# Attention with sign-weight feed-forward on one core: float32r rows for the feed-forward, another opening, and another share of the sums for GpSimd

## The chip, the cores and the metric

The kernel runs on one core of a Trainium2 chip. The metric is the device time of one execution in microseconds. A core has five engines that matter here: TensorE (PE in the profile), VectorE (DVE), ScalarE (ACT), GpSimd (POOL) and the queue engine SyncE (SP), which issues DMAs. Each works through its own instructions in order, and they wait for one another by semaphores. TensorE writes its products to eight banks of PSUM, and a bank is free again when the engine that reads it has finished.

## The reference

```python
def _L0_attn_ref(x, Wq, Wk, Wv):           # x: (4, 2048, 512), 16 heads of 32
    q = (x @ Wq.T).reshape(N, S, H, hd).transpose(0, 2, 1, 3)
    k = (x @ Wk.T).reshape(N, S, H, hd).transpose(0, 2, 1, 3)
    v = (x @ Wv.T).reshape(N, S, H, hd).transpose(0, 2, 1, 3)
    energy = jnp.einsum('nhqd,nhkd->nhqk', q, k)
    attn = jax.nn.softmax(energy / jnp.sqrt(jnp.float32(hd)), axis=3)
    out = jnp.einsum('nhql,nhld->nhqd', attn, v)
    return out.transpose(0, 2, 1, 3).reshape(N, S, D)

def _L0_ffn_ref(x, weights, scale, bias):
    w = (weights >= 0.0).astype(x.dtype) * 2.0 - 1.0
    y = jnp.einsum('bsi,oi->bso', x, w)
    y = y * scale + bias
    return jnp.clip(y, -100.0, 100.0)

x = _layernorm(x + _L0_attn_ref(x, Wq, Wk, Wv), axis=-1)
x = _layernorm(x + _L0_ffn_ref(x, weights, scale, bias), axis=-1)
```

Everything is float32. The feed-forward has the shape of one 512 x 512 matrix of signs, followed by a scale and a bias for each output column.

## The kernel before

**Work and steps.** A *group* `n` is one batch and four of the sixteen heads, so there are 16 groups, four to a batch. A *block* is 512 queries of one group (four blocks a group), and a *step* is one chunk of 128 keys for one block: 16 steps a block, 64 a group, 1024 in all. The program is one long list of steps, written out in full. In each step TensorE makes the scores of the chunk for four heads at once (`scores`, L300 and L306: first a bf16 product that puts minus the row maximum into the bank, then the f32 product of keys and queries), ScalarE takes exp (L313) into a tile `p` of 128 x 2048, and every second step TensorE multiplies two such tiles with the values (`weighted`, L324).

**Row maxima ahead.** The maxima are computed by a separate pass: `max_unit` (L248, L255, L267) makes the scores of 128 queries against 512 keys for four heads, and VectorE reduces each of the four banks to a maximum, the fourth one by way of a copy by ScalarE. One such unit stands in each step, for the step that comes `LEAD` = 22 steps later; sixteen units make a block's maxima, which `max_parts` collects and SP transposes by a DMA. So 22 units are done before the first scores.

**The denominators.** GpSimd adds up the tiles `p` of a block (`add_up`, L344): chunk 0 and 1 in its first instruction, then one chunk in each, up to chunk 14, so 14 additions a block. In `denominators` TensorE multiplies chunk 15 and then the sum of the other fifteen with a column of ones (`ones_times`, L350), which adds over the 128 keys. A tile `p` is taken from `ppool`, which has four buffers; a buffer is free when the value product and the addition have both read it. The very last block has a split of its own.

**Projections, feed-forward and finishing.** Into the odd steps a planner (`plan`) puts *big* tasks (pieces of the projections of the next group, L206, and pieces of the feed-forward) and *small* ones (transposes by TensorE); into the even steps it puts *col* tasks, such as the denominators. Each task has a first and a last step; the planner runs twice, the second time with the number of big tasks a group as a quota. In its units a piece of keys or queries weighs 2, a piece of values or feed-forward 1, and an odd step in the middle holds 2. Once a batch's attention is done, its rows are finished in the steps of the next batch (`Finish`): a first layer norm, `turn` (four transposes, L518, and ScalarE's copy, L524), `ffn` (L532 and three VectorE operations, L537, L538 and L540), a second layer norm and the store. The rows of the last batch are finished near the end (`finish_last`) and after it (`finish_end`). `take` and `give` keep a model of when each bank is free.

**The feed-forward.** The weights were turned into signs and multiplied with the scale before the start (`sign_weights`, GpSimd). A tile of 128 rows is done in three pieces of 172, 172 and 168 columns, each four f32 matmuls; in the last two blocks in one piece of 512.

**The opening.** Wk and Wq are loaded as a whole on ScalarE's queue and transposed; x comes tile by tile (128 rows, 256 KB) into a stage of three buffers on SP's queue, and each transpose issues the next load. Then come keys, queries and units, and Wv and the feed-forward weights are loaded meanwhile (`load_rest`).

Of the kernel before, what the change touches and what calls it, by code (L numbers as in the profile page):

```python
# [12 lines left out]
BF16 = mybir.dt.bfloat16  # L13
AF = mybir.ActivationFunctionType
# [6 lines left out]
def kernel(  # L21
# [13 lines left out]
    P = 128  # L35
# [14 lines left out]
    THIRDS = (0, 172, 344, D)  # L50
    W = 2 * P
    LEAD = NT + 6

# [4 lines left out]
    stage = ctx.enter_context(tc.tile_pool(name="stage", bufs=3))  # L58
    mpool = ctx.enter_context(tc.tile_pool(name="mpool", bufs=2))
    cpool = ctx.enter_context(tc.tile_pool(name="cpool", bufs=2))  # L60
# [5 lines left out]
    ppool = ctx.enter_context(tc.tile_pool(name="ppool", bufs=4))  # L66
# [54 lines left out]
    def load_weight(w, name):  # L121
        if name == "ws":
            raw = xpool.tile([P, DC, D], F32, tag="xg", name="raw_ws")
        else:
            raw = ppool.tile([P, DC, D], F32, tag="p", name=f"raw_{name}")
        rows = w.rearrange("(c p) i -> p c i", p=P)
        for cols in [slice(0, D)] if name in ("wv", "ws") else [ts(ic, P) for ic in range(DC)]:
            nc.scalar.dma_start(out=raw[:, :, cols], in_=rows[:, :, cols])
        return raw

    wT = {}

    def transpose_weight(name, ic):
        if ic == 0:
            wT[name] = const.tile([P, DC, D], F32, name=f"{name}T")
        i = take()
        pt = cols_of(i, DC, P)
        for oc in range(DC):
            nc.tensor.transpose(pt[:, oc, :], raws[name][:, oc, ts(ic, P)], ident)  # L139
        runs("full", 0.44)  # L140
        nc.scalar.copy(wT[name][:, ic, :].rearrange("p (c o) -> p c o", c=DC), pt)
        give(i, "ACT", 0.6)

    def sign_weights():

        ws = raws["ws"]
        nc.gpsimd.tensor_scalar(ws, ws, 0.0, 2.0, ALU.is_ge, ALU.mult)
        for oc in range(DC):
            nc.gpsimd.tensor_scalar(
                ws[:, oc, :], ws[:, oc, :], 1.0, scale_t[:, oc : oc + 1], ALU.subtract, ALU.mult  # L150
            )

    raws = {n: load_weight(w, n) for n, w in (("wk", wk), ("wq", wq))}
    scale_t = const.tile([P, DC], F32, name="scale_t")
    bias_bc = const.tile([P, D], F32, name="bias_bc")

    def load_rest():
        for n, w in (("wv", wv), ("ws", w_ffn)):
            raws[n] = load_weight(w, n)
        nc.sync.dma_start(out=scale_t, in_=ffn_scale.rearrange("(c p) -> p c", p=P))  # L160
        nc.sync.dma_start(out=bias_bc, in_=ffn_bias.partition_broadcast(P))
# [3 lines left out]
    xin = {}  # L165
# [14 lines left out]
    coming = [(b, g, j) for b in range(B) for g in range(NQB) for j in range(NTQ)]  # L180

    def load_x():
        if coming:
            b, g, j = coming.pop(0)
            xin[b, g, j] = stage.tile([P, D], F32, tag="xs", name="xs")
            nc.sync.dma_start(out=xin[b, g, j], in_=x[b, ds(g * QB + j * P, P), :])

    def transpose_x(b, g, j):
        if j == 0:
            xT[b, g] = xtpool.tile([P, DC, QB], F32, tag="xT", name=f"xT_{b}_{g}")  # L190
        xs = xin.pop((b, g, j))
        i = take()
        pt = cols_of(i, DC, P)
        for c in range(DC):
            nc.tensor.transpose(pt[:, c, :], xs[:, ts(c, P)], ident)  # L195
        runs("full", 0.44)
        nc.scalar.copy(xT[b, g][:, :, ts(j, P)], pt)
        give(i, "ACT", 0.6)
        load_x()
# [138 lines left out]

    def add_up(n, qb, kc, p, before):
        if kc == 1:  # L340
            acc[n, qb] = apool.tile([P, HG, QB], F32, tag="acc", name="acc")
        if 0 < kc < (NT // 2 if is_last(n, qb) else NT - 1):
            a = acc[n, qb]
            nc.gpsimd.tensor_tensor(a, before if kc == 1 else a, p, ALU.add)  # L344
        if kc == NT - 1:
            last_p[n, qb] = p
# [20 lines left out]
    def denominators(n, qb):  # L367
# [3 lines left out]
        else:  # L371
            b = take()
            ones_times(b, last_p.pop((n, qb)), True, False)
# [73 lines left out]
    class Finish:  # L447
# [66 lines left out]
        def turn(self, j):  # L514
# [5 lines left out]
            if self.b < B - 1:  # L520
                self.nT[j] = work.tile([P, DC, P], F32, tag="nT", name="nT")
            else:
                self.nT[j] = self.room[:, j, :].rearrange("p (c q) -> p c q", c=DC)
            nc.scalar.copy(self.nT[j], pt)  # L524
            give(i, "ACT", 0.6)

        def ffn(self, j, third):
            cols = slice(0, D) if third is None else slice(THIRDS[third], THIRDS[third + 1])
            i = take()
            py = ps[:, i, : cols.stop - cols.start]  # L530
            for c in range(DC):
                nc.tensor.matmul(  # L532
                    py, lhsT=self.nT[j][:, c, :], rhs=wT["ws"][:, c, cols],
                    start=(c == 0), stop=(c == DC - 1),
                )
            runs("full", 6.8e-3 * (cols.stop - cols.start))
# [4 lines left out]
            give(i, "DVE", 0.5 + 3.1e-3 * (cols.stop - cols.start))  # L541

        def make_room(self):

            if self.g < NQB // 2:
                t = kpool.tile([P, S], F32, tag="kT", name="room") if self.g == 0 else shared[0]
                shared[:] = [t]
                self.room = t.rearrange("p (j d) -> p j d", j=NTQ)
            else:
                self.room = xpool.tile([P, NTQ, D], F32, tag="xg", name="room")  # L550
# [30 lines left out]
    def finish(b, qb, a, every, w, lag):  # L581
# [6 lines left out]
        for j in range(NTQ):  # L588
# [3 lines left out]
            for k in range(3):  # L592
                task("big", t + 2, t + w, f.ffn, j, k, after=turned)
# [8 lines left out]
    def finish_last(qb, last):  # L602
# [5 lines left out]
        at(a + 1, f.make_room)  # L608
# [4 lines left out]
        for j in range(NTQ):  # L613
# [6 lines left out]
            for k in [None] if late else range(3):  # L620
                task("big", by if late else t + 2, by, f.ffn, j, k, after=turned)
# [8 lines left out]
    def finish_end(qb, last):  # L630
# [10 lines left out]
        at(total + 3, f.make_room)  # L641
# [12 lines left out]
    start = -LEAD - 5  # L654
    for ic in range(DC):
        task("small", -10, -2, transpose_weight, "wv", ic)
        task("small", 4, 60, transpose_weight, "ws", ic)
    at(-LEAD - 2, load_rest)
    at(-8, sign_weights)
    for n in range(N):  # L660
# [3 lines left out]
        for i in range(NQB):  # L664
# [3 lines left out]
            last = -LEAD + NTQ * i - (2 if i else 6) if n == 0 else first + (12, 12, 11, 8)[i]  # L668
# [7 lines left out]
        for t in range(NT):  # L676
            i, j = divmod(t, NTQ)
            after = turned[b, i, j]
            task("big", max(s0 - STEPS + 2, ready[i], -6), latest(i, s0 + t), project_v, n, t,
                 after=after)  # L680
            if j % 2 == 0:
                continue
            free = s0 - STEPS + 1 if n else start
            task("big", max(free, ready[i]), s0 - LEAD - 1 + i * (1 if n else NTQ),
                 project_k, n, t // 2, after=after)
            last = s0 + NT * i - LEAD + NTQ * (j - 1) - 1
            if n == 0 and i == 0:
                last = -LEAD - 2 + j
            task("big", max(s0 + NT * (i - 2), start), latest(i, last), project_q, n, t // 2,
                 after=after)  # L690
        for qb in range(NQB):
            first = s0 + NT * qb
            last = first + NT - 1
            ahead[first - 5] = n, qb
# [9 lines left out]
            if g == NG - 1:  # L704
# [3 lines left out]
                else:  # L708
                    (finish_end if is_last(n, qb) else finish_last)(qb, last)

# [6 lines left out]
    def plan(quota=None):  # L717
# [9 lines left out]
        while any(len(gone[kind]) < len(tasks[kind]) for kind in tasks):  # L727
# [5 lines left out]
            elif s % 2:  # L733
                most = {"small": 1, "big": 2}
# [46 lines left out]
    for _ in range(3):  # L781
        load_x()
    for name in ("wk", "wq"):
        for ic in range(DC):
            transpose_weight(name, ic)
# [6 lines left out]
    while s <= max(*chosen, *behind):  # L792
# [10 lines left out]
        later = None  # L803
        if 0 <= s + LEAD < total:
            n, at_n = divmod(s + LEAD, STEPS)
# [14 lines left out]
        if later is not None:  # L820
            later()
        if now is not None:
# [42 lines left out]
```

## Time and profile before

| | before |
|---|---|
| median of 3 runs | 4386.38 us (4384.66 to 4386.73) |
| profiled execution, its own time | 4386.25 us |
| its span, first to last instruction | 4384.5 us |
| mean granted TensorE clock | 0.998 |
| busy: PE, weight loads | 4345.0 us (99%), 2135.5 us (49%) |
| busy: DVE, ACT, POOL | 3315.9 us (76%), 2999.3 us (68%), 4083.3 us (93%) |
| GpSimd additions (L344) | 825 + 64, 4.54 us each |
| first scores (L300) start | 84.4 us |

The profile shows one execution. Its span is 1.75 us shorter than the same execution's time, and that time is within 0.2 us of the median. An f32 matmul leaves two records on TensorE, and so does its weight load; a bf16 matmul and a transpose leave one. The busy time of TensorE is not a measure of how well it works, because the ends of matmuls are modelled: how long a matmul really holds TensorE is read from one start to the next. In the chain of waits the pieces are laid end to end, so a group of matmuls there has about the time that it holds the engine.

### The profile page before, as it was taken

To read this page: it belongs to the slowest core of one execution; us is meant where nothing else is said; L and a number is where in the kernel's file an instruction comes from. 1 tells how busy PE (TensorE), PEld (TensorE's weight loads), DVE (VectorE), ACT (ScalarE), POOL (GpSimd) and SP (SyncE) were. 2 spreads that over 40 slices of the span, in tenths; PEclk is the share of its full clock that TensorE was granted. 3 is DMA by queue.
4 is the path that set the end of the run, shared out by engine and by line. 5 is a ranking of instruction groups with operands and counts; after the bars stand their busy time and mean duration, and the time that the engine had idled before them with its cause. 6 is when DMAs were issued, how large, how long until landed. Compare 5 with 4: busy or idle time off the path is not lost.

```text
span 4384.5 us, 89302 instructions
## 1 busy us (share of the span) xinstructions
PE 4345.0 (99%) x36092; PEld 2135.5 (49%) x36092; DVE 3315.9 (76%) x5908; ACT 2999.3 (68%) x6173; POOL 4083.3 (93%) x940
## 2 busy tenths in 40 slices
PE   9999999999999999999999999999999999999998
PEld 5444444444454454455445454455544545455443
DVE  6777777777777777777777777777777777777774
ACT  4666666676667667676676766767667676767665
POOL 3999999999999999999999999999999999999993
PEclk9999999999999999999999999999999999999999
DMA  2000000010001000011000100001100000001101
GB/s 88 11 10 14 11 14 10 12 39 22 21 13 27 13 23 20 11 45 36 21 20 11 33 10 21 23 10 49 25 20 21 20 21 23 20 11 33 24 23 49
DMA packets 263351, 101.41 MB, mean 23 GB/s; under 512 B 169372, under 2 KB 239004, under 8 KB 262936
## 3 DMA queue, kind: packets, MB, share of 16 engines
q1 hardware_dynamic: 257656, 91.50, 8.6%
q8 instruction: 282, 4.62, 0.4%
q10 hardware_dynamic: 5280, 4.19, 0.3%
q14 instruction: 133, 1.09, 0.1%
HBM read 54.26 MB, written 33.02 MB: 20 GB/s over the span
## 4 chain that ended last, share of the span: by engine, by line
PE 91%; POOL 6%; DVE 1%; ACT 1%; issue 1%; DMA 0%; ACTq 0%; POOLq 0%; DVEq 0%
PE ps L324 20%; PE ps L248 19%; PE ps L306 19%; PE ps L206 15%; PE ps L300 8%; POOL acc L344 6%; PE ps L532 5%; PE ps L350 3%; PE ps L391 1%; PE ps L195 1%; PE ps L518 1%; ACT p L313 1%; DVE part L255 1%; DMA xs<-in_L_attn_x_dram 0%; PE ps L139 0%
## 5 line engine op out<-in xcount | busy, mean ns | idle before, releaser
L344 POOL TENSOR_TENSOR acc<-acc,p 128x2048 f32<-128x2048 f32 x825 | 3743.7, 4538 | 102.8 <-ACT p L313 42.6
L313 ACT ACTIVATE p<-ps 128x512 f32<-128x512 f32 x4096 | 2114.8, 602 | 1136.0 <-PE ps L306 1108.2
L255 DVE TENSOR_REDUCE part<-ps 128x1 f32<-128x512 f32 x3072 | 1933.0, 683 | 774.6 <-PE ps L248 774.2
L248 PE MATMUL ps<-kT,qT 32*128 32x512 f32 x8192 | 1114.3, 590 | 0.2 <-DVE xg_last L434 0.2
L306 PE MATMUL ps<-qT,kT 32*128 32x512 f32 x8192 | 1073.3, 591 | 0.0
L324 PE MATMUL ps<-p,vv 128*32 128x512 f32 x8192 | 983.4, 598 | 1.8 <-ACT p L313 1.8
L248 PEld LDWEIGHTS ps<-kT,qT 32*128 32x128 f32 x8192 | 542.8, 184 | 381.0 <-issue 194.5
L255 DVE TENSOR_REDUCE part<-moved 128x1 f32<-128x512 f32 x1024 | 691.9, 676 | 3.3 <-ACT moved L267 3.2
L267 ACT COPY moved<-ps 128x512 f32<-128x512 f32 x1024 | 631.0, 616 | 22.1 <-PE ps L248 18.0
L324 PEld LDWEIGHTS ps<-p,vv 128*32 128x32 f32 x8192 | 220.2, 109 | 686.9 <-issue 345.9
L300 PE MATMUL ps<-negm,ones_bf 32*128 32x512 bf16 x4096 | 443.1, 384 | 4.9 <-ACT p L313 2.9
L306 PEld LDWEIGHTS ps<-qT,kT 32*128 32x128 f32 x8192 | 405.8, 184 | 44.3 <-issue 27.5
L336 DVE TENSOR_TENSOR oT<-ps,oT 128x512 f32<-128x512 f32 x448 | 309.7, 691 | 97.4 <-PE ps L324 59.2
L344 POOL TENSOR_TENSOR acc<-p 128x2048 f32<-128x2048 f32 x64 | 290.8, 4544 | 96.0 <-ACT p L313 95.8
L300 PEld LDWEIGHTS <-ones_bf 32*128 32x128 bf16 x4096 | 105.6, 91 | 551.0 <-issue 522.3
L206 PEld LDWEIGHTS ps<-wvT,xT 128*128 128x128 f32 x2048 | 250.9, 191 | 80.3 <-ACT p L313 75.6
L206 PE MATMUL ps<-wvT,xT 128*128 128x128 f32 x2048 | 279.2, 280 | 0.3 <-ACT p L313 0.2
L206 PE MATMUL ps<-xT,wqT 128*128 128x256 f32 x1024 | 248.8, 386 | 2.7 <-ACT p L313 2.7
L206 PE MATMUL ps<-xT,wkT 128*128 128x256 f32 x1024 | 248.7, 387 | 0.0
L206 PEld LDWEIGHTS ps<-xT,wkT 128*128 128x128 f32 x1024 | 184.9, 190 | 68.8 <-ACT p L313 47.0
L206 PEld LDWEIGHTS ps<-xT,wqT 128*128 128x128 f32 x1024 | 184.5, 190 | 66.6 <-ACT p L313 44.9
L532 PEld LDWEIGHTS ps<-wsT,nT 128*128 128x128 f32 x1152 | 167.8, 189 | 94.2 <-ACT p L313 93.3
(75 smaller groups left out, 1722.4 us busy)
## 6 DMA issues: line engine op xcount, KB each, us to landing
xs<-in_L_attn_x_dram SPq DMA_DIRECT2D x64, 256.0 KB
xc<-in_L_attn_x_dram SPq DMA_DIRECT2D x60, 256.0 KB
res<-xc SPq DMA_DIRECT2D x60, 256.0 KB
xg<-res SPq DMA_DIRECT2D x12, 1024.0 KB
out_dram<-xg SPq DMA_DIRECT2D x12, 1024.0 KB
xg_last<-res SPq DMA_DIRECT2D x4, 768.0 KB
out_dram<-xg_last SPq DMA_DIRECT2D x3, 1024.0 KB
raw_wk<-in_L_attn_Wk_dram ACTq DMA_DIRECT2D x4, 256.0 KB
```

Source lines behind the costliest of these rows:

```text
L206: nc.tensor.matmul(pp, lhsT=lhs(c), rhs=rhs(c), start=(c == 0), stop=(c == DC - 1))
L248: nc.tensor.matmul(ps[:, banks[h], :], lhsT=qT[n, qb][rows, ts(qc, P)], rhs=kT[n][rows, ts(kb, QB)], start=True, stop=True,)
L255: nc.vector.tensor_reduce(part[:, qc, h : h + 1, kb], src, AX.X, ALU.max, negate=True)
L267: nc.scalar.copy(moved, ps[:, banks[-1], :])
L300: nc.tensor.matmul(ps[:, banks[h], :], lhsT=ones_bf[rows, :], rhs=negm[n, qb][rows, :], start=True, stop=False,)
L306: nc.tensor.matmul(ps[:, banks[h], :], lhsT=kT[n][rows, ts(kc, P)], rhs=qT[n, qb][rows, :], start=False, stop=True,)
L313: nc.scalar.activation(p[:, h, :], ps[:, banks[h], :], AF.Exp, scale=SM_SCALE)
L324: nc.tensor.matmul(pb[cols, :], lhsT=vv[n][:, kc, cols], rhs=p[:, h, :], start=(i == 0), stop=(i == 1),)
L336: nc.vector.tensor_tensor(outs[n, qb], pb, outs[n, qb], ALU.add)
L344: nc.gpsimd.tensor_tensor(a, before if kc == 1 else a, p, ALU.add)
L350: nc.tensor.matmul(ps[h * HD : (h + 1) * HD, b, :], lhsT=ones, rhs=p[:, h, :], start=start, stop=stop,)
L532: nc.tensor.matmul(py, lhsT=self.nT[j][:, c, :], rhs=wT["ws"][:, c, cols], start=(c == 0), stop=(c == DC - 1),)
```

## The change

Five things change together.

1. **Feed-forward.** `turn` makes two tiles in float32r: ScalarE copies the transposed rows into `high`, and VectorE subtracts `high` from the same bank into `low`. `ffn` multiplies both with the weights, which are now pure signs in float32r, in two halves of 256 columns (one piece of 512 in the last two blocks): eight matmuls a half into one bank. The scale is a tile of its own and a fourth VectorE operation. The room that the last batch used for its turned rows goes.
2. **The sums.** In every second block of batches 1 to 3 GpSimd adds 13 chunk pairs instead of 14, and TensorE multiplies two single chunks with ones, not one. The very last block keeps its split.
3. **The opening.** The first 128 rows of Wk and Wq, then all 16 tiles of x of batch 0, are loaded at once, x into four of the buffers of `ppool`. The other rows of Wk, Wq and Wv come through the stage and are transposed in the group before they are needed.
4. **The lead.** 18 units, not 22, stand ahead of the first scores (`LEAD0`); in the first steps of the run every second step holds a second unit until the lead is 22 again. An odd step with a second unit holds one big task less.
5. **Buffers.** `ppool` has five, not four; `stage` two, not three; `cpool` (columns of x for the attention sum) one, not two.

```diff
-    THIRDS = (0, 172, 344, D)
+    HALF = D // 2
     LEAD = NT + 6
+    LEAD0 = NT + 2
-    stage = ctx.enter_context(tc.tile_pool(name="stage", bufs=3))
+    stage = ctx.enter_context(tc.tile_pool(name="stage", bufs=2))
-    cpool = ctx.enter_context(tc.tile_pool(name="cpool", bufs=2))
+    cpool = ctx.enter_context(tc.tile_pool(name="cpool", bufs=1))
-    ppool = ctx.enter_context(tc.tile_pool(name="ppool", bufs=4))
+    ppool = ctx.enter_context(tc.tile_pool(name="ppool", bufs=5))
...
+    def transpose_weight(name, g):
+        if g == 0:
+            wT[name] = const.tile([P, DC, D], F32, name=f"{name}T")
+        raw = xin.pop((name, g))
+        i = take()
+        pt = cols_of(i, DC, P)
+        for ic in range(DC):
+            nc.tensor.transpose(pt[:, ic, :], raw[:, ts(ic, P)], ident)
+        runs("full", 0.44)
+        nc.scalar.copy(wT[name][:, :, ts(g, P)], pt)
+        give(i, "ACT", 0.6)
+        if g:
+            load_next()
...
         nc.gpsimd.tensor_scalar(ws, ws, 0.0, 2.0, ALU.is_ge, ALU.mult)
-        for oc in range(DC):
-            nc.gpsimd.tensor_scalar(
-                ws[:, oc, :], ws[:, oc, :], 1.0, scale_t[:, oc : oc + 1], ALU.subtract, ALU.mult
-            )
+        nc.gpsimd.tensor_scalar(ws, ws, 1.0, 0.0, ALU.subtract, ALU.add)
...
+    def load_first():
+        first = ppool.tile([P, DC, D], F32, tag="p", name="first_w")
+        for i, name in enumerate(("wk", "wq", "wv")):
+            xin[name, 0] = first[:, i, :]
+        for name in ("wk", "wq"):
+            nc.scalar.dma_start(out=xin[name, 0], in_=rows_of[name][ds(0, P), :])
+        for g in range(NQB):
+            t = ppool.tile([P, NTQ, D], F32, tag="p", name="first_x")
+            for j in range(NTQ):
+                xin[0, g, j] = t[:, j, :]
+                nc.sync.dma_start(out=t[:, j, :], in_=x[0, ds(g * QB + j * P, P), :])
+
     def load_rest():
+        nc.scalar.dma_start(out=xin["wv", 0], in_=wv[ds(0, P), :])
+        raws["ws"] = xpool.tile([P, DC, D], F32, tag="xg", name="raw_ws")
+        nc.scalar.dma_start(out=raws["ws"], in_=w_ffn.rearrange("(c p) i -> p c i", p=P))
+        nc.sync.dma_start(out=scale_bc, in_=ffn_scale.partition_broadcast(P))
         nc.sync.dma_start(out=bias_bc, in_=ffn_bias.partition_broadcast(P))
...
+    def chunks_added(n, qb):
+        if is_last(n, qb):
+            return NT // 2
+        return NT - 1 if n < NG or qb % 2 == 0 else NT - 2
+
     def add_up(n, qb, kc, p, before):
-        if 0 < kc < (NT // 2 if is_last(n, qb) else NT - 1):
+        if 0 < kc < chunks_added(n, qb):
             a = acc[n, qb]
             nc.gpsimd.tensor_tensor(a, before if kc == 1 else a, p, ALU.add)
-        if kc == NT - 1:
-            last_p[n, qb] = p
+        elif kc >= NT - 2:
+            last_p[n, qb] = last_p.get((n, qb), []) + [p]
...
-            ones_times(b, last_p.pop((n, qb)), True, False)
+            for k, p in enumerate(last_p.pop((n, qb))):
+                ones_times(b, p, k == 0, False)
...
-            if self.b < B - 1:
-                self.nT[j] = work.tile([P, DC, P], F32, tag="nT", name="nT")
-            else:
-                self.nT[j] = self.room[:, j, :].rearrange("p (c q) -> p c q", c=DC)
-            nc.scalar.copy(self.nT[j], pt)
-            give(i, "ACT", 0.6)
+            high = work.tile([P, DC, P], F32R, tag="high", name="high")
+            low = work.tile([P, DC, P], F32R, tag="low", name="low")
+            nc.scalar.copy(high, pt)
+            spend("ACT", 0.6, clock["PE"] + 0.2)
+            nc.vector.tensor_tensor(low, pt, high, ALU.subtract)
+            give(i, "DVE", 0.7)
+            self.nT[j] = high, low
...
-        def ffn(self, j, third):
+        def ffn(self, j, half):
-            for c in range(DC):
-                nc.tensor.matmul(
-                    py, lhsT=self.nT[j][:, c, :], rhs=wT["ws"][:, c, cols],
-                    start=(c == 0), stop=(c == DC - 1),
-                )
-            runs("full", 6.8e-3 * (cols.stop - cols.start))
+            for k, part in enumerate(self.nT[j]):
+                for c in range(DC):
+                    nc.tensor.matmul(
+                        py, lhsT=part[:, c, :], rhs=wT["ws"][:, c, cols],
+                        start=(k == c == 0), stop=(k == 1 and c == DC - 1),
+                    )
+            runs("full", 3.4e-3 * wide)
+            nc.vector.tensor_tensor(py, py, scale_bc[:, cols], ALU.mult)
             nc.vector.tensor_tensor(py, py, bias_bc[:, cols], ALU.add)
...
-            ahead[first - 5] = n, qb
+            ahead[first - (5 if first else 2)] = n, qb
...
+    def units(s):
+        def first(s):
+            return min(max(s + min(LEAD0 + max(s, 0) // 2, LEAD), 0), total)
+
+        return range(first(s), first(s + 1))
...
-                most = {"small": 1, "big": 2}
+                most = {"small": 1, "big": 3 - len(units(s))}
```

## The prediction

> **What bounds the kernel now.** I read the page's busy rows first, then the chain of waits for two stretches apart (the first batch, and the three later ones), then the timeline for the pace of single instructions, and last the chain of the opening and of the end.
>
> The windows of batch 0 and of the next two (columns: stretch; length; busy time of PE, weight loads, DVE, ACT, POOL; clock, DMA):
>
> ```profile
> 84.00:1116.00 1032.00, 1024.62 (x8644) 484.45 (x8639) 764.13 (x1282) 705.87 (x1451) 1004.80 (x222) 1.00 0.07 17
> 1116.00:2187.00 1071.00, 1069.83 (x9028) 530.59 (x9023) 829.71 (x1485) 744.74 (x1531) 1026.51 (x233) 1.00 0.09 22
> 2187.00:3257.00 1070.00, 1069.52 (x9026) 530.43 (x9024) 829.79 (x1489) 746.70 (x1536) 1024.35 (x233) 1.00 0.09 22
> ```
>
> Each row is one batch, 16 blocks of 16 steps: a block takes 64.5 us in batch 0 and 66.9 us later. PE is busy all but 1 us of a later batch, at full clock, but POOL is above 95% too. The chain tells them apart (first line: 110 to 1116 us, second: 1116 to 4250 us):
>
> ```profile
> by line: POOL acc L344 24.9%; PE ps L324 16.6%; PE ps L306 15.6%; PE ps L248 15.3%; PE ps L206 14.2%; PE ps L300 6.8%; PE ps L350 2.4%; issue 1.6%; ACT p L313 1.0%; PE ps L195 0.9%; PE ps L391 0.8%; PE ps L139 0.1%; POOLq L344 0.1%
> by line: PE ps L324 21.8%; PE ps L248 21.1%; PE ps L306 20.3%; PE ps L206 15.7%; PE ps L300 8.2%; PE ps L532 6.6%; PE ps L350 2.8%; PE ps L518 0.9%; PE ps L391 0.8%; PE ps L195 0.6%; ACT p L313 0.6%; POOL acc L344 0.4%; issue 0.1%; DVE part
> ```
>
> Batch 0, which has no feed-forward, is held by POOL and PE together; later POOL is 0.4% of the chain and everything is TensorE. There, TensorE time taken away is time won, as far as POOL allows; feed-forward (L532) is 6.6% of that stretch.
>
> The pace of one matmul is read from starts in the timeline, since ends are modelled:
>
> ```profile
> 2001.71 0.40 PE L300 MATMUL ps<-negm,ones_bf 32*128 32x512 bf16 x4
> ...
> 2001.93 1.03 PE L306 MATMUL ps<-qT,kT 32*128 32x512 f32 x8
> ...
> 2008.14 0.60 PE L195 MATMUL ps<-ident,xs 128*128 128x128 f32 x4
> ...
> 2008.58 1.69 PE L206 MATMUL ps<-xT,wqT 128*128 128x256 f32 x7
> ```
>
> The bf16 group has one record to a matmul and the next group starts 0.22 us on: 512 columns in one pass. Four f32 transposes take 0.44 us, 0.11 each for 128 columns. The end of the run gives f32 at full width, two records to a matmul:
>
> ```profile
> 4330.67 3.60 PE L532 MATMUL ps<-wsT,room 128*128 128x512 f32 x8
> ...
> 4343.01 7.03 PE L532 MATMUL ps<-wsT,room 128*128 128x512 f32 x16
> ```
>
> Eight more records cost 3.43 us: 0.43 a record, 0.86 us a matmul. So f32 costs two records of two passes each, four times the bf16 pass.
>
> **The change part by part.** *Feed-forward matmuls.* Before, a tile is 12 matmuls of 172 or 168 columns, 24 records; at 0.84 ns a column a record that is 4 x 2 x (0.146 + 0.146 + 0.143) = 3.47 us. The chain has one whole tile, with its switches:
>
> ```profile
> 3490.47 3.67 PE ps L532 x24
> ```
>
> After, a tile is 2 halves x 2 parts x 4 = 16 matmuls of 256 columns in float32r. No float32r runs in this trace. Lower bound: the bf16 pace, 256 columns in 0.109 us, so 1.75 us a tile. Upper bound: the f32 form, two records of 0.214, so 6.85 us. I take the bf16 pace: [...]here each operand is already rounded to one part (the signs are exact, the rows come as high and low), so one pass each is the nearest row. The planner's cost in the diff says the same (3.4e-3 us a column for eight matmuls), and its counterpart of before, 6.8e-3, agrees with the trace. Saved: 1.72 us a tile. Tiles on the dense path are 48 of batches 0 to 2 and the 8 of the last batch's first two blocks: 56 x 1.72 = **-96 us**.
>
> A rule speaks against this. The row: f32 transposes, one record each, take 0.11 us for 128 columns, half the bf16 rate. The Trainium skill (Perfetto Trace Analysis, Engine Utilization) halves TensorE's output rate for a form it calls FP32_LOW_HIGH. If float32r ran at that rate, a matmul of 256 columns would take 0.214 and a tile 3.43 us, and the -96 would be -2. But the transposes' 0.11 us may as well be the load of their 128 weight columns: the same skill (TensorE: Matmul & The Clock Gate, LDWEIGHTS) gives a load as columns / 1.2 ns, 107 ns here. By that rule 16 loads are 1.71 us, still under the 1.75 of the matmuls. The trace's single-pass load lasts longer, in the page as given by form:
>
> ```profile
> L195 PEld LDWEIGHTS ps<-ident,xs 128*128 128x128 f32 x256 | 27.4, 140 | 36.6 <-ACT p L313 27.3 <-ACT kT L210 3.0 <-issue 2.4
> ```
>
> 140 ns, yet a new one starts every 110, so loads overlap. Were they to queue at 140, a tile would be 2.24 us and the saving 28 us smaller.
>
> *TensorE takes a chunk from GpSimd.* In odd blocks of groups 4 to 15, except the very last block (23 blocks), one more set of four sums with ones runs: 8 records, 0.86 us (16 are 1.72 in the chain near the end). 23 x 0.86 = **+20 us** on the dense path. POOL loses 23 adds of 4.54 us, 104 us in all. This earns nothing by today's chain; but with feed-forward halved a block on 14 adds would stand at 65.2 us of PE against 63.6 of POOL, 98%, where batch 0 stands now. It is cover, paid for with 0.43 us a block.
>
> *Vector work of a tile.* Added: the low part, a 512-wide subtract from PSUM (0.69, as the L430 row), and a scale multiply in each half. Three operations on thirds are about 0.34 each, 3.0 us a tile; four on halves, between 0.337 at 172 and 0.696 at 512, are 0.43 each, 3.4 us. With the subtract, +1.1 us a tile, 17 us a batch: DVE goes from 830 of 1071 to about 847 of 1050, 81%. The subtract waits for ScalarE's copy of the high part, which stands behind four exps and the moved copy; behind it in DVE's queue stands the row maximum of that copy, and TensorE waits for the banks. The steps' slack in DVE covers this: its waits for L248 sum to 528 us from 1116 to 4250. If that cover goes, some 0.3 us for each of 48 turns: 15 us. I take **+4 us**. The ScalarE copy only changes its type.
>
> *The opening.* Before, the chain is:
>
> ```profile
> 24.34 9.17 DMA xs<-in_L_attn_x_dram
> ...
> 57.03 19.77 DVE part L255 x33
> 78.13 7.12 DVE part L255 x12
> ```
>
> First scores come at 84.4 us. Wk and Wq, 2 MB, stand ahead of most of x; then Wv and the feed-forward weights, another 2 MB, delay x again at 24 us. After, two pieces of 256 KB go first on the ScalarE queue, while SP issues all 16 tiles of x at about 0.4 us each, and the rest of the weights comes behind. In the first 28 us the DMAs moved 178 GB/s at 0.67 busy, so 4.5 MB take some 17 to 25 us, and x is eaten over 40. Transposes of x start at about 6 us, not 13, and the 3.0 us that TensorE waits for x go: about 8 to 10 us. The tail is VectorE's: 45 maxima in 27 us, 0.6 each, 2.4 us for a unit of four. Eighteen units, not 22, stand ahead of the first scores: -9.5 us. SP's transposing load of the first maxima now has two such steps, 4.8 us, and landed 2.2 us after its issue. First scores at about 66: **-18 us** (-8 to -25).
>
> *Batch 0 takes what was moved.* Nine weight transposes (0.44 each) and four units (0.86 and a switch each) are 8 us of PE over batch 0, where POOL's 14 adds of 4.55, 63.7 of 64.5 us, stand beside them. The fifth p buffer lets POOL lag further: ScalarE waited 17.8 us for POOL there. Together **-2 us** (-10 to +6). The staging and column buffers lose one each; a staged tile has two steps (8 us) until the next turn and a column four steps between its store and the next load, so SP's queue, on which the maxima's loads stand, should not stop. If it does, the scores wait behind it; I price it within the range.
>
> *The end.* Three feed-forward tiles of 3.4 us in the last 55 us lie on the chain and halve; the multiply and subtract add 0.7 each on DVE, which then paces the last four tiles. **-4 us** (-8 to +3).
>
> Sum: -96 + 20 + 4 - 18 - 2 - 4 = -96 us against the profiled execution's own 4386.25 us (span 4384.5), which is within 0.2 us of the median: **4290 us**.
>
> **The rivals.** *Loads set the pace* (140 ns): 4290 + 28 = 4318. For it: a matmul of 256 columns in one pass is shorter than a load. Against: transposes at 110.
>
> *The opening and VectorE give nothing:* x in one burst delays Wv, and the low parts hold DVE's queue: +18 and +15, 4323.
>
> *float32r at half rate:* -2 in place of -96 and nothing at the end: about 4388, no change that can be told.
>
> *Slower: float32r runs in f32's form*, two records of 0.214. Place: each tile's matmuls; price 6.85 - 3.47 = 3.38 us x 56 = +189, and some 13 in the end: about 4590. The change turns slower when one such matmul takes over 0.21 us. For it: the trace shows no float32r at all[...]. In this case, too, the planner's belief and the machine part, and the extra sums are pure cost.
>
> **How the numbers follow.** The likeliest case has 0.67, loads 0.12, opening and VectorE 0.08, half rate 0.07 (0.04 same, 0.03 slower by DVE's additions), f32 form 0.06. Some 0.2% (9 us) is what a measurement of this kernel can tell. Faster 0.87, same 0.04, slower 0.09. The range 4262 to 4340 takes the first three cases with their bounds (-28 to +50), about 0.8.
>
> **What the profile after would show.** Right: L532's successor with one record to a matmul, 16 to a tile, starts 0.11 us apart; later batches at about 65.5 us a block with PE above 99% and POOL at about 92 to 96%; batch 0 still near 64.4 with POOL in the chain; first scores near 66 us; 568 + 184 = 752 records of L350's sums on single chunks. Wrong: starts 0.21 apart or two records (rates), starts at 0.14 (loads), DVE or ACT as releasers ahead of PE in later batches, first scores after 78 us, or POOL with over 10% of the chain in later batches.

## The result, and the profile after

The changed kernel is slower: 4407.59 us (median; 4405.41 to 4408.52) against 4385.63 us for the kernel before on the same chip, ratio 1.0049, 95% interval 1.0038 to 1.0060. Its profiled execution took 4405.41 us, with a span of 4403.6 us against 4384.5. The forecast was 96 us faster.

The matmul part of the change did what it should, and the time went elsewhere. The chain of waits of the changed kernel from 1109 us (start of batch 1) to 4260 us, to be read against the second chain line of before (L275 is now the max units, L570 the feed-forward, L383 the sums with ones, L333 and L327 the scores):

```profile
by line: PE ps L275 22.5%; PE ps L351 21.5%; PE ps L333 20.0%; PE ps L233 15.8%; PE ps L327 8.5%; PE ps L570 3.4%; PE ps L383 3.4%; ACT p L340 1.2%; PE ps L552 0.9%; PE ps L425 0.8%; POOL acc L377 0.6%; PE ps L221 0.5%; DVE part L282 0.3%; 
```

Feed-forward fell from 6.6% to 3.4%, and TensorE is still nearly all of the chain. But the max units, whose work is the same, rose from 21.1% to 22.5%. The windows of batches 1 and 2 show the same from the other side:

```profile
1109.00:2188.70 1079.70, 1079.03 (x8957) 518.60 (x8953) 844.99 (x1486) 741.16 (x1528) 995.23 (x226) 1.00 0.09 22
2188.70:3268.30 1079.60, 1079.32 (x8964) 518.93 (x8960) 845.71 (x1488) 744.85 (x1537) 988.14 (x225) 1.00 0.09 22
```

A batch takes 1079.7 us where it took 1071; TensorE's busy share is as full as before, VectorE has 845 us of work as forecast, GpSimd some 30 us less. "PE busy" hides the loss, since a group of matmuls that has started and waits for a bank in its middle counts as busy here. It shows when one counts from each start to the next. By function, in us over the whole run (the last feed-forward group to the end of its last matmul):

| start to start, us | before | changed |
|---|---|---|
| max units | 1053 | 1125 |
| scores | 1148 | 1165 |
| feed-forward | 243 | 144 |
| sums with ones | 118 | 141 |

One step in the timeline shows where the 72 us of the max units come from. Before, a third of a tile, then the next step's max unit (L248):

```profile
1999.48 1.41 PE L532 MATMUL ps<-wsT,nT 128*128 128x168 f32 x8
2001.38 0.33 DVE L537 TENSOR_TENSOR ps<-ps,bias_bc 128x168 f32<-128x168 f32 x1
...
2002.12 0.33 DVE L540 TENSOR_TENSOR xg<-xg,ps 128x168 f32<-128x168 f32 x1
...
2002.79 1.03 PE L248 MATMUL ps<-kT,qT 32*128 32x512 f32 x8
```

VectorE lets the bank go at 2002.45, and 0.34 us later the max unit asks for it. After, a half:

```profile
2328.88 0.74 PE L570 MATMUL ps<-wsT,high 128*128 128x256 f32 x4
2329.46 0.64 PE L570 MATMUL ps<-wsT,low 128*128 128x256 f32 x4
...
2330.78 0.42 DVE L575 TENSOR_TENSOR ps<-ps,scale_bc 128x256 f32<-128x256 f32 x1
...
2332.01 1.75 PE L275 MATMUL ps<-kT,qT 32*128 32x512 f32 x8
...
2332.17 0.42 DVE L579 TENSOR_TENSOR xg<-xg,ps 128x256 f32<-128x256 f32 x1
...
2332.65 0.29 PEld L275 LDWEIGHTS ps<-kT,qT 32*128 32x128 f32 x2 [0.44 <-DVE xg L579]
```

The four operations hold the bank until 2332.59. The max unit starts three of its heads at 2332.01 and waits for the fourth bank: its last weights load at 2332.65, with L579 as the releaser, and it takes 1.75 us instead of 1.03. With four banks in the scores and four asked for by the max unit, all eight are needed at this point of every step. Over the whole run the weight loads of the max units (first before, then after) come to wait for L579; VectorE as a releaser was one of the prediction's signs of being wrong:

```profile
L248 PEld LDWEIGHTS ps<-kT,qT 32*128 32x128 f32 x8192 | 542.8, 184 | 381.0 <-issue 194.5 <-ACT vv L210 24.5 <-DVE part L255 17.1
...
L275 PEld LDWEIGHTS ps<-kT,qT 32*128 32x128 f32 x8192 | 568.1, 184 | 430.0 <-issue 207.2 <-DVE xg L579 28.0 <-ACT p L340 21.2
```

Over batches 1 and 2, a max unit behind a step with a feed-forward piece and a value piece lasts 0.963 us from its start to the next work in the kernel before, and 1.573 us in the changed one; behind a turn and a piece of a projection 0.969 and 1.252.

The opening: first scores come at 70.8 us, not 84.4.

### The profile page after: what moved, and what is told of

Same layout as the page of the kernel before. It is cut to its first block, busy times and chain, and to the rows that moved or that the text cites. A ratio compares the mean times of both kernels' runs of the same rounds, so it can differ in the third digit from the quotient of the medians.

```text
span 4403.6 us, 88631 instructions
## 1 busy us (share of the span) xinstructions
PE 4351.3 (99%) x35828; PEld 2086.9 (47%) x35828; DVE 3381.5 (77%) x5924; ACT 2994.5 (68%) x6173; POOL 3979.4 (90%) x914
## 4 chain that ended last, share of the span: by engine, by line
PE 93%; POOL 2%; DVE 2%; ACT 2%; issue 0%; DMA 0%; ACTq 0%; POOLq 0%; DVEq 0%; SPq 0%
PE ps L275 21%; PE ps L351 21%; PE ps L333 19%; PE ps L233 16%; PE ps L327 8%; PE ps L383 3%; PE ps L570 3%; POOL acc L377 2%; ACT p L340 1%; PE ps L425 1%; PE ps L221 1%; DVE part L282 1%; PE ps L552 1%; DVE st L516 0%; DVE ps L576 0%
## 5 line engine op out<-in xcount | busy, mean ns | idle before, releaser
L377 POOL TENSOR_TENSOR acc<-acc,p 128x2048 f32<-128x2048 f32 x802 | 3640.1, 4539 | 124.9 <-ACT p L340 66.9
L340 ACT ACTIVATE p<-ps 128x512 f32<-128x512 f32 x4096 | 2114.9, 602 | 1150.6 <-PE ps L333 1143.8
L282 DVE TENSOR_REDUCE part<-ps 128x1 f32<-128x512 f32 x3072 | 1933.4, 683 | 660.5 <-PE ps L275 659.8
L275 PE MATMUL ps<-kT,qT 32*128 32x512 f32 x8192 | 1190.4, 592 | 2.0 <-ACT p L340 1.7
L333 PE MATMUL ps<-qT,kT 32*128 32x512 f32 x8192 | 1084.0, 594 | 0.0
L275 PEld LDWEIGHTS ps<-kT,qT 32*128 32x128 f32 x8192 | 568.1, 184 | 430.0 <-issue 207.2
L282 DVE TENSOR_REDUCE part<-moved 128x1 f32<-128x512 f32 x1024 | 692.5, 676 | 0.4 <-ACT moved L294 0.4
L327 PE MATMUL ps<-negm,ones_bf 32*128 32x512 bf16 x4096 | 458.2, 384 | 11.6 <-DMA negm<-split 3.9
L333 PEld LDWEIGHTS ps<-qT,kT 32*128 32x128 f32 x8192 | 406.2, 184 | 53.5 <-issue 37.5
L327 PEld LDWEIGHTS <-ones_bf 32*128 32x128 bf16 x4096 | 106.4, 91 | 558.3 <-issue 521.3
L361 DVE COPY oT<-ps 128x512 f32<-128x512 f32 x64 | 44.3, 692 | 150.8 <-PE ps L351 150.8
```

What stands on the lines that cost most here:

```text
L275: nc.tensor.matmul(ps[:, banks[h], :], lhsT=qT[n, qb][rows, ts(qc, P)], rhs=kT[n][rows, ts(kb, QB)], start=True, stop=True,)
L282: nc.vector.tensor_reduce(part[:, qc, h : h + 1, kb], src, AX.X, ALU.max, negate=True)
L327: nc.tensor.matmul(ps[:, banks[h], :], lhsT=ones_bf[rows, :], rhs=negm[n, qb][rows, :], start=True, stop=False,)
L333: nc.tensor.matmul(ps[:, banks[h], :], lhsT=kT[n][rows, ts(kc, P)], rhs=qT[n, qb][rows, :], start=False, stop=True,)
L340: nc.scalar.activation(p[:, h, :], ps[:, banks[h], :], AF.Exp, scale=SM_SCALE)
```

## The experiments

Each result is given with the ratio to the kernel before on the same chip.

**One more operation in the kernel before.** A bank of a third is held 0.34 us longer; nothing else differs.

```diff
+            nc.vector.tensor_tensor(py, py, one_bc[:, cols], ALU.mult)
             nc.vector.tensor_tensor(py, py, bias_bc[:, cols], ALU.add)
```

> The kernel before with one more VectorE operation on each feed-forward third (a multiply by ones in the bank), so that the bank is held for four operations of 0.34 us, 1.36 us, not three. Bank theory: max units behind a feed-forward piece rise above 0.96 us by 0.1 to 0.3 in 144 of them, 15 to 40 us, 4400 to 4425. Rival (the wait comes from the feed-forward piece being 0.3 us shorter on TensorE, so that the max unit comes earlier): under 8 us, about 4390.

4415.33 us, ratio 1.0069 (1.0056 to 1.0081): 29 us slower. Max units behind a third and a value piece rose from 0.963 to 1.112 us. The hold grew by one operation with the gap before it, some 0.37 us, and the max units by 0.149. By this estimate the room is some 0.2 us, less than the 0.34 us that the timeline shows between release and start.

**The multiply left out of the changed kernel.**

```diff
-            nc.vector.tensor_tensor(py, py, scale_bc[:, cols], ALU.mult)
```

> The changed kernel without the multiply by the scale (the output lacks the scale): a bank is held for three operations, 1.3 us. Bank theory: the wait of the max unit behind a feed-forward piece falls by up to 0.43 us, from 1.57 to about 1.2, the time by some 35 us to about 4372, less than with the bank freed after one operation though VectorE has 27 us less to do. Rival (VectorE's load): more is won than with the bank freed early, since only here VectorE has less work.

4365.55 us, ratio 0.9954 (0.9942 to 0.9966): 42 us less than the changed kernel, and max units behind feed-forward and a value piece at 1.180 us. The output lacks the scale. This alone doesn't part the bank from VectorE's load.

**The same, with VectorE's work put back where it holds no bank.**

```diff
-            nc.vector.tensor_tensor(py, py, scale_bc[:, cols], ALU.mult)
...
             nc.vector.tensor_tensor(dst, dst, py, ALU.add)
+            idle = small.tile([P, 1], F32, tag="idle", name="idle")
+            nc.vector.tensor_reduce(idle, scale_bc[:, cols], AX.X, ALU.max, negate=True)
```

> The changed kernel without the multiply in the bank (the output lacks the scale), but with an operation of the same length for VectorE, a maximum over the scale's columns in SBUF, behind the last operation of each half, where the bank is already free. VectorE has the work of the changed kernel, the bank is held for three operations. Bank theory: as without the multiply, 4365 (within 6). Rival (VectorE's load): back to the changed kernel's 4407.

4371.16 us, ratio 0.9967 (0.9955 to 0.9980). The group of the added operation:

```profile
L581 DVE TENSOR_REDUCE idle<-scale_bc 128x1 f32<-128x256 f32 x112 | 46.1, 412 | 0.0
```

It is about as long as the multiply was (423 ns), yet 36 of the 42 us stay won, and max units behind feed-forward stay at 1.184 us. So 36 us come from holding the bank. The other 6 are no more than the two intervals can tell apart; of the 4.1 us between the two profiled executions 2.9 lie behind the last scores.

**14 additions on GpSimd everywhere.**

```diff
-        return NT - 1 if n < NG or qb % 2 == 0 else NT - 2
+        return NT - 1
```

> The changed kernel with 14 additions on GpSimd in every block, and so one single chunk on TensorE. Theory: the 23 additional sets of sums are pure cost on TensorE while other waits keep a block at 67.4 us, above GpSimd's 63.7: 20 us less, about 4388. Rival (GpSimd would bind): no gain, or slower, with GpSimd as the releaser of ScalarE and over 10% of the chain in later batches.

4386.05 us, ratio 1.0000 (0.9992 to 1.0008): 21.5 us less than the changed kernel. The extra sums were pure cost, and of the size forecast.

**The opening alone,** on the kernel before, with its f32 feed-forward and 14 additions (also the lead, the buffers and the weights by rows).

```diff
     LEAD = NT + 6
+    LEAD0 = NT + 2
...
+        for g in range(NQB):
+            t = ppool.tile([P, NTQ, D], F32, tag="p", name="first_x")
```

> The kernel before with the opening, the lead, the buffers and the weights by rows of the change, but its f32 feed-forward in thirds, its scaled weights and 14 additions. Theory: the first scores come 13 us earlier (84.4 to 71), batch 0 gives back 6 us (its first block 72.7 for 66.4), the rest is as before: about 4379. Rival (buffers lost in the stage and the columns cost waits in the later batches): later blocks over 66.9 us and no gain, 4386 or more.

4377.58 us, ratio 0.9982 (0.9974 to 0.9990): 7.6 us won. First scores at 71.7 us; batch 0 takes 1038.3 us where it took 1031.7, its first block 72.7 for 66.4; later batches take 1069 to 1070 for 1071. The smaller stage and column buffers cost nothing that shows. From here to the 14-addition kernel, the float32r feed-forward has taken 95 us out of TensorE's feed-forward (240 to 145) and put 80 into the max units (1044 to 1124) and 17 into the scores. In all it is 8.5 us slower by the medians, 11.5 between the two profiled executions; the projection pieces (3 us) and the stretch behind the last scores (2 us) are longer too.

**The value product ahead of the max unit,** in even steps behind a feed-forward piece or a turn, with 14 additions.

```diff
+        if s % 2 == 0 and held and 0 < s < total and any(
+            t[3].__name__ in ("ffn", "turn") for t in chosen[s - 1]
+        ):
+            weighted(held)
+            held = []
```

> The changed kernel with 14 additions everywhere, and in an even step behind a step with a feed-forward piece or a turn the value product (1.85 us) comes ahead of the max unit, so that the bank of the feed-forward has 1.85 us more until the max unit asks for it; VectorE's work and the bank's hold are unchanged. Bank theory: max units behind feed-forward go back to 0.96 us and the time falls by 50 to 70 us below the 4386 of the 14-addition kernel, to about 4330. Rival: the eight banks are short in any order, and the value product or the next scores wait instead: 4375 or more.

The theory missed, and the rival (the banks are short in any order) held: 4423.82 us, ratio 1.0088 (1.0074 to 1.0101), 38 us slower than the kernel it was made from. The max units it was meant for did recover, to 1.008 us behind feed-forward and 0.963 behind turns. But now the max unit of the odd step follows at once, and 70 of those in batches 1 and 2 last 1.956 us. The weight loads of the max units there wait for VectorE's row maxima (L282, 77 us in batches 1 and 2), which still read the banks of the max unit before. The wait moved to the next shortage of banks; the order of the step wasn't free slack.

**One operation only.** Scale, bias and clip left out, 14 additions, so that the bank is held 0.42 us.

```diff
-            nc.vector.tensor_tensor(py, py, scale_bc[:, cols], ALU.mult)
-            nc.vector.tensor_tensor(py, py, bias_bc[:, cols], ALU.add)
-            nc.vector.tensor_scalar(py, py, MAX_VAL, -MAX_VAL, ALU.min, ALU.max)
```

> The changed kernel with 14 additions everywhere and without the multiply, the bias and the clip (the output lacks scale, bias and clip): a bank of the feed-forward is held for one operation of 0.42 us. Bank theory: max units behind feed-forward fall to 0.96 us; of the 80 us that max units last longer in the 14-addition kernel than with the opening alone (1124 for 1044), all but the part behind turns (0.29 for each of 64, 19 us) goes: about 4386 - 60 = 4325. Rival (what three operations left, 1086 for 1044, has another cause): it stays at the 4344 of the kernel with the bias on TensorE, less the 15 us of its matmuls, 4330 at most 4 below; then the max units behind feed-forward stay near 1.16.

4324.07 us, ratio 0.9857 (0.9844 to 0.9871), as expected to 1 us. Max units behind feed-forward and a value piece take 0.956 us, no more than before; those behind turns stay at 1.252. The run is 54 us below the opening alone, although the turns' wait and the scores' 17 us are still there; 8 of the 54 lie behind the last scores, where the operations left out are simply gone. VectorE also has less to do here, so this run alone does not part the bank from VectorE's load; the run with GpSimd mostly idle, below, has the same 0.956 us with all four operations. Blocks of batches 1 and 2 then take 66.0 us with GpSimd on 14 additions.

**The bank freed after one operation, all four kept.** The first writes to SBUF, the other three work there; the row's buffers at the end are packed closer for room.

```diff
-            nc.vector.tensor_tensor(py, py, scale_bc[:, cols], ALU.mult)
-            nc.vector.tensor_tensor(py, py, bias_bc[:, cols], ALU.add)
+            nc.vector.tensor_tensor(y, py, scale_bc[:, cols], ALU.mult)
+            nc.vector.tensor_tensor(y, y, bias_bc[:, cols], ALU.add)
```

> The changed kernel, but the first VectorE operation of each feed-forward half writes its product to a tile in SBUF, so that the bank is free after one operation (0.42 us) and not after four (1.7 us); VectorE's work is the same. Theory (the bank): in the changed kernel a max unit that follows a feed-forward piece lasts 1.57 us from start to next start, where it took 0.96 before, about 60 us over three batches; it should fall back to under 1.05 and the time to about 4350. Rival (VectorE's queue is simply longer): the maxima come as late as before, max units stay near 1.5 and the time stays within 8 us of 4407.

5027.34 us, ratio 1.1464 (1.1449 to 1.1480): neither theory. The groups by form show where the time went:

```profile
L327 PE MATMUL ps<-negm,ones_bf 32*128 32x512 bf16 x4096 | 509.0, 393 | 452.3 <-DVE part L282 428.1 <-DVE y L579 15.6 <-DMA negm<-split 3.9
...
L583 DVE TENSOR_SCALAR y<-y 128x256 f32<-128x256 f32 x112 | 306.1, 2733 | 3.8
L582 DVE TENSOR_TENSOR y<-y,bias_bc 128x256 f32<-128x256 f32 x112 | 297.6, 2657 | 3.8
...
L585 DVE TENSOR_TENSOR xg<-xg,y 128x256 f32<-128x256 f32 x96 | 193.2, 2013 | 3.4
...
L579 DVE TENSOR_TENSOR y<-ps,scale_bc 128x256 f32<-128x256 f32 x112 | 46.8, 417 | 9.8 <-PE ps L570 4.5 <-issue 4.4
```

With one operand in PSUM the operation takes 417 ns on average; with all in SBUF 2013 to 2733. TensorE waits 428 us for the row maxima (L282), which stand behind these operations in VectorE's queue. Of the 320 operations in the three slow groups 193 take over 1 us, and each of these starts while a GpSimd addition runs and ends 0.15 to 0.29 us after it. The granted clock was 0.94 in this run, 0.996 in the changed kernel, so not all of the 620 us between them need be this wait. A test without most of those additions followed.

**The same, with GpSimd mostly idle.** From group 4 on only the first addition of each block is made (denominators leave out chunks).

```diff
-            nc.gpsimd.tensor_tensor(a, before if kc == 1 else a, p, ALU.add)
+            if kc == 1 or n < NG or is_last(n, qb):
+                nc.gpsimd.tensor_tensor(a, before if kc == 1 else a, p, ALU.add)
```

> The kernel with the bank freed after one operation (5027), in which from group 4 on GpSimd makes only the first of its additions in each block (the output's denominators leave out chunks). In the 5027 kernel VectorE's operations with both operands in SBUF (y with the bias, 128x256) took 2657 ns instead of 433, and their ends follow the end of a GpSimd addition by 0.28 us. Theory (they wait until GpSimd's addition is over): with GpSimd idle for most of each block they take about 430 ns and the time falls to under 4380. Rival (two operands in SBUF are slow in themselves): they stay near 2.6 us and the time near 5000.

4378.91 us, ratio 0.9984 (0.9977 to 0.9991). The three groups:

```profile
L583 DVE TENSOR_TENSOR y<-y,bias_bc 128x256 f32<-128x256 f32 x112 | 157.3, 1405 | 3.8
...
L584 DVE TENSOR_SCALAR y<-y 128x256 f32<-128x256 f32 x112 | 41.3, 369 | 3.9
L586 DVE TENSOR_TENSOR xg<-xg,y 128x256 f32<-128x256 f32 x96 | 40.9, 426 | 3.3
```

Two are back at 369 and 426 ns. The first is still slow on average, because 33 of its 112 meet an addition that is left, as in the timeline:

```profile
1515.39 4.55 POOL L378 TENSOR_TENSOR acc<-p 128x2048 f32<-128x2048 f32 x1 [61.95 <-ACT p L340]
1515.86 0.41 DVE L580 TENSOR_TENSOR y<-ps,scale_bc 128x256 f32<-128x256 f32 x1
1516.31 3.92 DVE L583 TENSOR_TENSOR y<-y,bias_bc 128x256 f32<-128x256 f32 x1
```

The addition ends at 1519.94, the VectorE operation at 1520.23. And max units behind feed-forward and a value piece are at 0.956 us here, and all max units together at 1073 us as with one operation, with all of VectorE's four operations in place: the bank, once more.

**The bias on TensorE.** A version with the whole result: 14 additions; bias divided by scale, in three bf16 parts in three rows of a tile of zeros, goes into the bank by one bf16 matmul with ones, and VectorE's addition goes.

```diff
+            nc.tensor.matmul(py, lhsT=ones_bf, rhs=bias3[:, cols], start=True, stop=False)
             for k, part in enumerate(self.nT[j]):
...
-            nc.vector.tensor_tensor(py, py, bias_bc[:, cols], ALU.add)
```

> The changed kernel with 14 additions everywhere, and the bias divided by the scale put into the bank by TensorE (one bf16 matmul of 256 columns with three parts of it in three rows) in place of VectorE's addition: three operations hold the bank, as without the scale. Bank theory: the 42 us that leaving out the multiply won, less 128 matmuls of 0.11 us, 14: about 28 us below the 14-addition kernel's 4386, 4358, faster than the kernel before. Rival (the wait is not set by the bank's hold): 4386 + 14 = 4400.

4344.57 us, ratio 0.9907 (0.9892 to 0.9923): faster than both kernels, 41.5 us below the 14-addition one. The added matmuls cost less than the 14 us allowed for: feed-forward is at 146.5 us, 2 more. Max units behind feed-forward are at 1.162 us, so a part of the wait is left. GpSimd is busy for 94% of this span and 0.3% of the chain of later batches:

```profile
PE 4299.1 (99%) x35764; PEld 2078.8 (48%) x35764; DVE 3337.1 (77%) x5805; ACT 2993.5 (69%) x6173; POOL 4092.1 (94%) x947
...
by line: PE ps L295 22.3%; PE ps L371 22.0%; PE ps L353 20.5%; PE ps L253 16.2%; PE ps L347 8.7%; PE ps L591 3.1%; PE ps L403 2.8%; ACT p L360 0.9%; PE ps L572 0.9%; PE ps L445 0.8%; PE ps L588 0.7%; PE ps L241 0.5%; POOL acc L397 0.3%; iss
```

(The first line is from the page, the second is the chain from 1109 to 4200 us.)

**Both parts of a turned row on VectorE,** on that version.

```diff
-            nc.scalar.copy(high, pt)
+            nc.vector.tensor_copy(high, pt)
             nc.vector.tensor_tensor(low, pt, high, ALU.subtract)
```

> The kernel with 14 additions and the bias on TensorE (4344.6), with both parts of the turned rows made by VectorE (copy to high, then the subtract), so that VectorE doesn't wait for ScalarE's copy, which stands behind four exps. Theory: the bank of the turn is free earlier, max units behind a turn fall from 1.25 to near 1.0, 64 of them, 10 to 19 us: about 4330. Rival (VectorE's 0.69 us more for each turn costs what the wait did): 4340 to 4350.

Slower than both forecasts: 4357.07 us, ratio 0.9931 (0.9918 to 0.9945), 12.5 us slower. Max units behind a turn rose from 1.252 to 1.457 us on average. These averages mix two kinds. In batches 1 and 2, 16 of the 32 turns share their step with a piece of keys or queries, and the max unit hardly waits (0.96 us before, 0.96 to 1.07 now); 16 share it with a shorter value piece, and there the max unit took 1.55 us and now takes 1.93. One of these, with the bias on TensorE:

```profile
1274.30 1.89 DVE L302 TENSOR_REDUCE part<-ps 128x1 f32<-128x512 f32 x3 [0.65 <-PE ps L295]
...
1276.57 0.69 DVE L579 TENSOR_TENSOR low<-ps,high 128x512 fp32r<-128x512 f32 x1 [0.38 <-ACT high L577]
...
1277.31 0.30 PEld L295 LDWEIGHTS ps<-kT,qT 32*128 32x128 f32 x4 [0.31 <-DVE low L579]
```

And the same step with both parts on VectorE:

```profile
1276.09 0.68 DVE L577 CAST high<-ps 128x512 fp32r<-128x512 f32 x1
...
1276.80 0.69 DVE L578 TENSOR_TENSOR low<-ps,high 128x512 fp32r<-128x512 f32 x1
```

The wait for ScalarE's copy was there, 0.38 us, and it went. But the copy that replaces it takes VectorE 0.68 us behind the same three maxima, so the subtract ends at 1277.49 and not at 1277.26, and the bank is held longer. This is what the rival said, at a higher price.

## Why the prediction was wrong

**What failed is the term "+4" for the vector work of a tile.** That step of the forecast asked whether VectorE has the time, found 528 us of waiting in it, and called that the cover. What ran out was the time of a bank. The change lengthens the hold from 1.07 us (2001.38 to 2002.45) to 1.81 (2330.78 to 2332.59), and there was 0.34 us at most until the max unit asked for it, some 0.2 by the run with one operation more. The prediction had named the banks, but behind the subtract only, and priced them at 0.3 us for 48 turns; the 112 feed-forward halves of the dense path, held by a fourth operation and by pieces 256 wide, had no price at all. Measured from opening alone to the 14-addition kernel, max units took 80 us more, where +4 was forecast. Some 19 of it lie behind turns (64 times 0.29), and 52 went when the bank was held for one operation (1124 to 1072). The forecast missed by 118 us; this one term is about 76 of it, the scores' 17 us (cause open, below) and the opening's 12 are the next. The rival "the opening and VectorE give nothing" came nearest to the place: it saw banks held by VectorE's queue, but at the turns alone, with 15 us for them. "Slower" had been given its 0.09 for rates of float32r that did not come.

**The matmuls were right.** float32r runs as one record a matmul, in the groups by form 448 for each part. Behind the first of a group (0.22 us) records start 0.116 to 0.121 us apart, slower than the 0.109 taken, far from 0.214 and under the 0.140 of the loads' rival, although a weight load here lasts 190 ns in the profile. A half takes 1.06 us to the next work where a third took 1.27, so a tile takes 2.12 us and took 3.81. Both are some 0.35 us above the forecast's sums (1.75 and 3.47), and that the two errors cancel is luck. On the dense path feed-forward lost 92 us where 96 were forecast, and 7 at the end. Neither the half rate that the Trainium skill gives for FP32_LOW_HIGH (Perfetto Trace Analysis, Engine Utilization) nor the queue of loads came true.

**The extra sums:** +20 forecast, 21.5 measured. What was wrong is their use as cover: with 14 additions at 66.0 and 66.4 us a block (one operation; bias on TensorE), GpSimd did not bind. No run came down to the 65.2 us for which the cover was meant.

**The opening:** 18 forecast, 13.6 measured in the changed kernel for the first scores, 12.7 alone; SP's transposing load now stands in the chain there (2.5 us from 68.3). Batch 0 gave back 6.6 us where a gain of 2 was taken: the units that are moved behind the first scores lengthen its first block by 6.3 us. That GpSimd has not yet fallen behind at that time, and so hides none of it, is argued and was not tried. Opening and batch 0 together were put at 20 us; the opening alone is worth 7.6.

**The end:** -4 forecast, none found. From the last scores to the end of the span it is 55.5 us before and 55.3 after.

**What stays open:** 17 us more in the scores' own groups with float32r, which stayed with one operation too. 11 of them lie in the last batch and 7 in batches 1 and 2, most of these 7 behind odd steps with projection pieces only, of which there are more (108, before 86) since feed-forward fills fewer steps; why those steps wait 0.1 us was not tried. And 10 max units in batches 1 and 2, behind a step with feed-forward alone, last 1.96 us in the changed kernel and also with one operation. In both, the releaser of their last weight loads is ScalarE's exp (L340, a wait of 0.70 us) and not the feed-forward's last operation. In the two kernels that take the later operations to SBUF they last 0.95 to 1.10 us, and 0.963 with the value product ahead; which bank that is stays open.

## What to carry to other kernels

When a matmul gets shorter by moving work behind it to the engine that empties the bank, price the bank too, not only the engine: hold time against the time until the next work needs it, read in the timeline of one step. The Trainium skill says to evacuate promptly (PSUM — Partial Sum Buffer, Summary: rules for kernel authors); here 0.43 us of hold on 112 pieces was worth 36 us with VectorE's work unchanged. A reordering that relieves one point only helps if the next one has banks to spare.

## What the runs showed of the hardware

A VectorE operation with both operands in SBUF, if it starts while GpSimd works through an addition of 128 x 2048 (4.54 us), waits for the end of it: 2657 ns on average in place of about 425, ending 0.28 to 0.29 us after the addition. So does the in-place tensor_scalar in SBUF, 2733 ns with 293 at best, which ends 0.15 us after it. The Trainium skill names the cause (GPSIMD Engine Reference, Specifications: SBUF interfaces shared with VectorE, in contention with its operations of two SBUF inputs or in a 2-port mode); these runs agree for two inputs, and in which mode the tensor_scalar ran no view shows. The kernel in which VectorE met these additions was 620 us slower than the changed one. Maxima over one SBUF tile (412 ns for 256 columns with the operation put back, 676 for 512 everywhere) and operations with one operand in PSUM (417 ns) were not touched. So in this kernel, where GpSimd is busy, the operations were better left in the bank, and fewer of them was the way to free it.
